# Moving the last stage's weights and images into memory that the routing tables held, and gating its first image in halves

## The chip, the cores and the metric

The program runs on one core of one Trainium2 chip. A core has TensorE (PE in the profile; its weight loads are listed apart as PEld), VectorE (DVE), ScalarE (ACT), GpSimd (POOL) and SyncE (SP), each with its own stream of instructions that it works off in order. They share the on-chip memories SBUF and PSUM, and transfers between SBUF and the device's main memory are made by DMA engines, on orders that SP, ACT or POOL issue. The metric is the device time of one execution in microseconds (us); lower is better.

## What is computed

Two layers follow one another on x of shape (32, 128, 56, 56), in float32.

Layer 0 is a depthwise 7x7 convolution, a normalisation over the channels, and a mixture of 8 experts with 2 experts for each token (a pixel of an image) and a limited number of tokens for each expert. Layer 1 weighs each image with gates along rows and columns, convolves it 3x3 and ends in a SiLU. Cut to what matters here:

```python
# layer 0: x -> depthwise conv -> normalise -> experts
logits = xf @ Wg + bg
topv, topi = jax.lax.top_k(logits, 2)
# each expert takes at most cap = 1.25 * T / 8 tokens, by priority
h = gelu(einsum('ecd,edf->ecf', eb, W1) + b1)
y = einsum('ecf,efd->ecd', h, W2) + b2
x = input + x_skip + layer_scale * moe

# layer 1: gates along h and w, then a 3x3 convolution
x_h = x.mean(3) + x[..., :w // 2].mean(3) + x[..., :w // 4].mean(3)
x_w = x.mean(2) + x[:, :, :h // 2].mean(2) + x[:, :, :h // 4].mean(2)
y = h_swish(bn1d(einsum('ncl,mc->nml', concat([x_h, x_w], 2), w1) + b1))
a_h = sigmoid(einsum('nml,cm->ncl', y[:, :, :h], wh) + bh)
a_w = sigmoid(einsum('nml,cm->ncl', y[:, :, h:], ww) + bw)
out = conv3x3(x * a_w * a_h, wc) + bc
out = out * s2 + (be2 - m2 * s2)
return out * sigmoid(out)
```

## The kernel before

The kernel is written with a framework that lays tiles into memory pools, finds the waits between instructions itself, and orders the instructions of each engine within a stretch of code without branches by its own estimate. A tile of a later pool may lie where a tile of a closed pool was; an instruction that writes it then has to wait until everything that used the old tile is done. So where a tile lies decides how early it can be filled, and the order in the source is not always the order on an engine.

The stages follow one another:

1. The depthwise convolution (line 144), 0 to about 680 us.
2. Normalisation, logits and gates for each token (line 227 and on), to about 1170 us. Each token gets a row in the buffer `acc_d` in main memory.
3. Routing and the experts, to about 3318 us. For each expert a routing of 49 steps on DVE and PE (class `Routing`, lines 370 to 550) finds which rows it takes. Its tables lie in the pool `rc`: work tables for two routings at a time, and for every expert four small results that the experts read later (`new_idx`, line 653). The routing of the later experts is woven into the work of the earlier ones; its last steps are in the fourth expert. An expert works on up to 31 blocks of 512 rows, cut into five chunks (`CHUNKS`). For a block, POOL gathers rows by indirect DMA (line 591), PE transposes them (602), DVE copies them out of PSUM (604), PE multiplies by W1 (612), ACT applies the GELU (613), PE multiplies by W2 (621), ACT and DVE form the rows to be stored (632 to 641), and POOL scatters them to `acc_d` (646). Scatters of a chunk are issued during the next one, gathers one chunk ahead. Chunks after the first stand in a branch that depends on how many rows the expert takes. The weights of expert e + 1 are loaded by SP at the start of expert e (659, 661).
4. The last stage, from about 3318 us to the end. After the last scatter comes a fence: 16 small DVE memsets (line 790), each on a tile that a scatter reads, and every load from `acc_d` waits for them. SP's queue then holds the loads of the weights (`wc` at 820, `w1t` at 835, `wht`, `wwt`, the vectors at 814), the first x (883) and the rows of `acc_d` (891). DVE forms six weight sets `wk` from `wc`, because the 3x3 convolution is done in a transformed way that computes four output rows from six combinations of input rows.

The last stage works on pairs of images. A pair is 49 tiles of 128 tokens, taken in seven groups of seven tiles. `combine` loads the two rows of each token from `acc_d` (`cxn` and `cx`), POOL adds them (894), PE transposes them (900) and DVE adds them to x (902). `squeeze` (915 to 918) reduces each half of an image for the gates. `attend` computes the gates (925 to 945), DVE multiplies the image by them (948, 949) into one of two padded images, `pads`, and POOL and ACT form the six combinations `v` of its rows (956 to 967). `conv` (977 to 990) convolves half an image: 18 matmuls on PE, their combination on DVE, the SiLU and the store on ACT. The convolutions of a pair are spread over the groups of the pair after it. `attend` of the first image comes after the fourth group, that of the second after the seventh.

These pools matter: `cc` holds weights and, before, the two pads; `cx` two buffers for x; `ck` three each for `cxn` and `cx`; `cv` two for `v`.

Of the kernel before, what the change touches and what calls it, by code (L numbers as in the profile page):

```python
# [8 lines left out]
F32 = mybir.dt.float32  # L9
I32 = mybir.dt.int32  # L10
# [3 lines left out]
ALU = mybir.AluOpType  # L14
# [10 lines left out]
P = 128  # L25
NT = T // P
NPAIR = N // 2
# [18 lines left out]
def bc(ap, shape):  # L46
    return ap.to_broadcast(shape)
# [3 lines left out]
def moe_conv_then_coordatt_kernel(ctx: ExitStack, tc: tile.TileContext, a: dict, out: bass.AP):  # L51
# [260 lines left out]
    with ExitStack() as st:  # L312
# [251 lines left out]
        xsp = st.enter_context(tc.tile_pool(name="fs", bufs=2))  # L564
        ptp = st.enter_context(tc.tile_pool(name="fpt", bufs=1, space=PSUM))
# [87 lines left out]
        def new_idx(e):  # L653
            return [rc.tile([P, ST], I32, name=f"idx0_{e}"), rc.tile([P, ST], F32, name=f"idx1_{e}"),
                    rc.tile([1, 1], I32, name=f"taken_{e}"), rc.tile([1, NC_], I32, name=f"parts_{e}")]
# [138 lines left out]
    with ExitStack() as st:  # L794
        cp1 = st.enter_context(tc.tile_pool(name="cc", bufs=1))
        xp = st.enter_context(tc.tile_pool(name="cx", bufs=2))
        kp = st.enter_context(tc.tile_pool(name="ck", bufs=3))
# [36 lines left out]
        nc.gpsimd.memset(w1t, 0.0)  # L834
# [4 lines left out]
        for k in range(4):  # L839
            nc.gpsimd.memset(wq[:, k : k + 1], quarter[k])  # L840
# [14 lines left out]
        def folded(g, be, mean, v, b, n):  # L855
# [5 lines left out]
            nc.gpsimd.memset(mh, -0.5)  # L861
# [12 lines left out]
        for k in range(2):  # L874
            t = cp1.tile([C, H + 2, W + 2], F32, name=f"pad{k}")
            nc.gpsimd.memset(t, 0.0)
            pads.append(t)
# [3 lines left out]
        def load_pair(i):  # L881
            x1 = xp.tile([C, 2, HW], F32, tag="x1", name=f"x1_{i}")
            nc.sync.dma_start(x1, a["x"][2 * i : 2 * i + 2].rearrange("n c h w -> c n (h w)"))
            return x1
# [35 lines left out]
        def attend(i, im, x1):  # L920
# [26 lines left out]
            inner = pad[:, 1 : H + 1, 1 : W + 1]  # L947
            nc.vector.tensor_tensor(img, img, bc(aw.unsqueeze(1), [C, H, W]), ALU.mult)
            nc.vector.tensor_tensor(inner, img, bc(ah.unsqueeze(2), [C, H, W]), ALU.mult)  # L949

            v = vp.tile([C, 6, GR, W + 2], F32, tag="v", name=f"v{nm}")
            d = hp.tile([C, GR, 4, W + 2], F32, tag="d", name=f"d{nm}")
            byq = lambda x: x.rearrange("c (g r) w -> c g r w", r=4)
            low, high = byq(pad[:, 0:H, :]), byq(pad[:, 2 : H + 2, :])
            t = hp.tile([C, GR, 2, W + 2], F32, tag="t", name=f"t{nm}")
            nc.scalar.mul(t, low[:, :, 1:3, :], 4.0)
            nc.gpsimd.tensor_tensor(d, high, low, ALU.subtract)  # L957
            twice = hp.tile([C, GR, W + 2], F32, tag="twice", name=f"twice{nm}")
            nc.scalar.mul(twice, d[:, :, 1, :], 2.0)
            nc.scalar.mul(d[:, :, 0:2, :], d[:, :, 0:2, :], 4.0)  # L960
            nc.gpsimd.tensor_tensor(t, high[:, :, 1:3, :], t, ALU.subtract)
            nc.gpsimd.tensor_tensor(v[:, 1], t[:, :, 1, :], t[:, :, 0, :], ALU.add)  # L962
            nc.gpsimd.tensor_tensor(v[:, 2], t[:, :, 1, :], t[:, :, 0, :], ALU.subtract)
            nc.gpsimd.tensor_tensor(v[:, 3], d[:, :, 2, :], twice, ALU.add)
            nc.gpsimd.tensor_tensor(v[:, 4], d[:, :, 2, :], twice, ALU.subtract)
            nc.gpsimd.tensor_tensor(v[:, 0], d[:, :, 2, :], d[:, :, 0, :], ALU.subtract)
            nc.gpsimd.tensor_tensor(v[:, 5], d[:, :, 3, :], d[:, :, 1, :], ALU.subtract)
            return v
# [25 lines left out]
        todo = []  # L994
        for i in range(NPAIR + 1):
            x1 = load_pair(i) if i < NPAIR else None
# [75 lines left out]
```

## Time and profile before

| What | us |
|---|---|
| median of six runs | 4515.82 (4510.91 to 4523.32) |
| the profiled execution | 4507.24 |
| its span, first to last instruction | 4505.5 |
| experts' stage, first scatter order to last | 1390.1 to 3316.1 |
| first sum of `cxn` and `cx` | 3336.25 |
| first matmul of the last convolution | 3378.44 |
| one pair of the last stage, once settled | about 70.4 |

Busy time over the whole span: PE 3622.5 us (80%), PEld 2351.6 (52%), DVE 2567.3 (57%), POOL 2554.5 (57%), ACT 1410.8 (31%). These shares are means over stages with different limits. From 3400 us to the end PE was busy for 1036.8 of 1105.5 us; in the experts' stage, 1346 to 3308, for 1501.0 of 1962; between 3308 and 3336 not at all. The mean granted clock of PE was 0.89 of full speed.

Lines of the timeline read: start, duration, engine, source line, operation, output and inputs, shapes, number of instructions merged, and in brackets the idle time of the engine just before with what ended it. All times are in us from the start of the span. SPq is SP's queue of DMA orders: its duration is the time of issuing, not of the transfer.

### The profile page before, as it was taken

To read this page: it belongs to the slowest core of one execution; us is meant where nothing else is said; L and a number is where in the kernel's file an instruction comes from. 1 tells how busy PE (TensorE), PEld (TensorE's weight loads), DVE (VectorE), ACT (ScalarE), POOL (GpSimd) and SP (SyncE) were. 2 spreads that over 40 slices of the span, in tenths; PEclk is the share of its full clock that TensorE was granted. 3 is DMA by queue.
4 is the path that set the end of the run, shared out by engine and by line. 5 is a ranking of instruction groups with operands and counts; after the bars stand their busy time and mean duration, and the time that the engine had idled before them with its cause. 6 is when DMAs were issued, how large, how long until landed. Compare 5 with 4: busy or idle time off the path is not lost. (4 is left out here: it accounts for less than half of the span.)

```text
span 4505.5 us, 59987 instructions
## 1 busy us (share of the span) xinstructions
PE 3622.5 (80%) x21360; PEld 2351.6 (52%) x21360; DVE 2567.3 (57%) x5914; ACT 1410.8 (31%) x3132; POOL 2554.5 (57%) x1983
## 2 busy tenths in 40 slices
PE   9999997676318897797788546597858999999999
PEld 4444447666316665565566335465634444544544
DVE  1111115888866966876742212232347888888886
ACT  1111115555203343244243223243412333333332
POOL 1000002322217777668677537777769877877775
PEclk9999998787658898798889778798979999999999
DMA  9999995545362121111111111111155565555652
GB/s 166 222 229 217 229 198 196 214 201 221 149 244 57 49 58 52 45 45 46 52 51 56 50 30 52 56 55 57 56 169 176 168 196 177 182 195 166 196 160 77
DMA packets 814971, 587.33 MB, mean 130 GB/s; under 512 B 545984, under 2 KB 751312, under 8 KB 802128
## 3 DMA queue, kind: packets, MB, share of 16 engines
q1 hardware_dynamic: 508816, 328.72, 25.3%
q10 hardware_dynamic: 262336, 157.84, 12.5%
q0 software_dynamic: 43264, 94.64, 7.3%
q8 instruction: 193, 3.16, 0.3%
q14 instruction: 362, 2.97, 0.2%
HBM read 320.96 MB, written 260.09 MB: 129 GB/s over the span
## 5 line engine op out<-in xcount | busy, mean ns | idle before, releaser
L591 POOL DMA_INDIRECT xg<-acc_d,idx x676 | 673.9, 997 | 406.9 <-issue 181.3
L646 POOL DMA_INDIRECT acc_d<-yo,row x676 | 718.5, 1063 | 234.4 <-issue 81.9
L612 PE MATMUL ph<-fxt,w 128*128 128x512 f32 (+1 forms) x1440 | 700.1, 630 | 53.4 <-ACT ht L613 53.4
L613 ACT ACTIVATE ht<-ph,bias 128x512 f32<-128x512 f32 (+1 forms) x720 | 489.4, 682 | 707.5 <-PE ph L612 706.5
L977 PE MATMUL pc<-v,wk 128*128 128x392 f32 x1920 | 701.0, 507 | 0.4 <-POOL v L962 0.4
L621 PEld LDWEIGHTS py<-w,ht 128*128 128x128 f32 x5728 | 666.8, 193 | 64.8 <-issue 58.2
L621 PE MATMUL py<-w,ht 128*128 128x128 f32 x5728 | 672.4, 277 | 0.0
L144 PE MATMUL acc<-xt,band 56*64 56x424 f32 (+3 forms) x7168 | 668.7, 529 | 2.7 <-POOL band L132 2.7
L977 PEld LDWEIGHTS pc<-v,wk 128*128 128x128 f32 x1920 | 346.8, 191 | 305.9 <-issue 101.1
L144 PEld LDWEIGHTS acc<-xt,band 56*64 56x64 f32 x7168 | 320.3, 133 | 350.4 <-issue 277.5
L227 PE MATMUL lnps<-proj,lnyt 128*128 128x136 f32 x1568 | 354.7, 400 | 138.3 <-ACT sq L232 71.8
L612 PEld LDWEIGHTS ph<-fxt,w 128*128 128x128 f32 x1440 | 279.3, 206 | 328.7 <-issue 241.9
L636 ACT ACTIVATE yo<-xg,own 128x137 f32<-128x137 f32 x716 | 238.1, 401 | 630.0 <-DVE own L632 389.4
L227 PEld LDWEIGHTS lnps<-proj,lnyt 128*128 128x128 f32 x1568 | 349.4, 319 | 144.1 <-ACT sq L232 74.5
L157 DVE TENSOR_SCALAR yt<-acc,dwb 128x448 f32<-128x448 f32 x128 | 87.5, 684 | 584.4 <-PE acc L144 467.2
L639 DVE TENSOR_TENSOR ys<-py,b 128x512 f32<-128x512 f32 (+2 forms) x184 | 123.8, 675 | 491.6 <-PE py L621 481.7
L602 PE MATMUL pt<-ident,xg 128*128 128x128 f32 x716 | 137.1, 312 | 327.4 <-issue 152.2
L132 POOL COPY band<-hk 56x392 f32<-56x392 f32 x128 | 65.3, 510 | 574.4 <-issue 528.2
L987 DVE SCALAR_TENSOR_TENSOR y<-pc,y 128x392 f32<-128x392 f32 x640 | 317.5, 554 | 11.8 <-PE pc L977 11.8
L957 POOL TENSOR_TENSOR d<-pad 128x3248 f32<-128x3248 f32 x32 | 228.0, 7124 | 155.6 <-DVE pad L949 155.6
L894 POOL TENSOR_TENSOR cxn<-cxn,cx 128x896 f32<-128x896 f32 x112 | 260.5, 2334 | 68.2 <-DMA cxn<-acc_d 30.5
L602 PEld LDWEIGHTS pt<-ident,xg 128*128 128x128 f32 x716 | 97.3, 162 | 354.1 <-issue 297.8
(225 smaller groups left out, 4650.9 us busy)
## 6 DMA issues: line engine op xcount, KB each, us to landing
xt<-in_x SPq DMA_DIRECT2D x128, 392.0 KB
y_d<-yt ACTq DMA_DIRECT2D x256, 196.0 KB
lnyt<-y_d SPq DMA_DIRECT2D x16, 3136.0 KB
x<-in_x SPq DMA_DIRECT2D x16, 3136.0 KB
cxn<-acc_d SPq DMA_DIRECT2D x112, 448.0 KB
cx<-acc_d SPq DMA_DIRECT2D x112, 448.0 KB
out<-y ACTq DMA_DIRECT2D x64, 784.0 KB
acc_d<-xn SPq DMA_DIRECT2D x16, 1712.5 KB
```

The source lines that it names most:

```text
L144: nc.tensor.matmul(acc[c][half * G : (half + 1) * G, :, lo:hi], lhsT=band[rows, dw, :], rhs=xt[rows, im, lo + s : hi + s], start=(n == 0), ...
L227: nc.tensor.matmul(ps[:, j, :], lhsT=yf[:, self.j0 + g + j, :], rhs=proj, start=True, stop=True)
L591: d = nc.gpsimd.indirect_dma_start(out=xg[0:n, k, :], out_offset=None, in_=acc_d[0:T1, :], in_offset=bass.IndirectOffsetOnAxis(ap=idx[0][0 ...
L602: nc.tensor.transpose(pt[:, k * P : k * P + n], xg[0:n, k, 0:C], ident[0:n, 0:n])
L612: nc.tensor.matmul(ph[:, 0:N_], lhsT=w[0][:, f * P : (f + 1) * P], rhs=xt[:, 0:N_], start=True, stop=True)
L613: nc.scalar.activation(ht[:, f, 0:N_], ph[:, 0:N_], AF.Gelu, bias=w[2][:, f : f + 1])
L621: nc.tensor.matmul(py[0:n, k, :], lhsT=ht[:, f, k * P : k * P + n], rhs=w2[:, f, :], start=(f == 0), stop=(f == NF - 1))
L636: nc.scalar.activation(yo[0:n, k, :], xg[0:n, k, :], AF.Copy, scale=own[0:n, k : k + 1])
L646: d = nc.gpsimd.indirect_dma_start(out=acc_d[:, :], out_offset=bass.IndirectOffsetOnAxis(ap=row[0:n, k : k + 1], axis=0), in_=yo[0:n, k, : ...
L894: nc.gpsimd.tensor_tensor(xn, xn, x2, ALU.add)
L977: nc.tensor.matmul(m[k], lhsT=wk[k][:, dw, :], rhs=v[:, k, rows, dw : dw + W], start=(dw == 0), stop=(dw == 2))
L987: nc.vector.scalar_tensor_tensor(r[x], m[k], f, r[y_], ALU.mult, ALU.add)
```

## The change

Four things are changed.

- The four small results of a routing move from the pool `rc` to a pool of their own, `fi`, opened after the pools of the experts. The pads move from `cc` to a pool of their own, `cp`, between x and the rows of `acc_d`. With that, `cc` and `cx` lie where the routing's tables and its priorities were, and no longer where the experts' buffers or results are.
- Memsets of the last stage move from POOL to DVE, and only what no other instruction writes is cleared: of `w1t` the columns behind the loaded ones, of each pad its four edges.
- x is asked for a pair ahead: the first pair before the loop, and pair i + 1 at the start of iteration i. There are two buffers for x, as before.
- For the first image of the first pair, the two multiplications by the gates and all that POOL and ACT do for `v` are cut in two halves of output rows (29 and 27 rows of the image, 7 groups of four rows each). For that image the source also has the part from `t` ahead of the differences `d`; for all others the order is as before.

```diff
+        ixp = st.enter_context(tc.tile_pool(name="fi", bufs=1))
...
         def new_idx(e):
-            return [rc.tile([P, ST], I32, name=f"idx0_{e}"), rc.tile([P, ST], F32, name=f"idx1_{e}"),
-                    rc.tile([1, 1], I32, name=f"taken_{e}"), rc.tile([1, NC_], I32, name=f"parts_{e}")]
+            return [ixp.tile([P, ST], I32, name=f"idx0_{e}"), ixp.tile([P, ST], F32, name=f"idx1_{e}"),
+                    ixp.tile([1, 1], I32, name=f"taken_{e}"), ixp.tile([1, NC_], I32, name=f"parts_{e}")]
...
+        padp = st.enter_context(tc.tile_pool(name="cp", bufs=1))
...
-        nc.gpsimd.memset(w1t, 0.0)
+        nc.vector.memset(w1t[:, MIP:QP], 0.0)
...
-            nc.gpsimd.memset(wq[:, k : k + 1], quarter[k])
+            nc.vector.memset(wq[:, k : k + 1], quarter[k])
...
-            nc.gpsimd.memset(mh, -0.5)
+            nc.vector.memset(mh, -0.5)
...
-            t = cp1.tile([C, H + 2, W + 2], F32, name=f"pad{k}")
-            nc.gpsimd.memset(t, 0.0)
+            t = padp.tile([C, H + 2, W + 2], F32, name=f"pad{k}")
+            for edge in (0, H + 1):
+                nc.vector.memset(t[:, edge, :], 0.0)
+            for edge in (0, W + 1):
+                nc.vector.memset(t[:, 1 : H + 1, edge : edge + 1], 0.0)
...
-            inner = pad[:, 1 : H + 1, 1 : W + 1]
-            nc.vector.tensor_tensor(img, img, bc(aw.unsqueeze(1), [C, H, W]), ALU.mult)
-            nc.vector.tensor_tensor(inner, img, bc(ah.unsqueeze(2), [C, H, W]), ALU.mult)
...
+            first = (i, im) == (0, 0)
+            cuts = (0, RP, GR) if first else (0, GR)
+            rows_done = 0
+            for g0, g1 in zip(cuts, cuts[1:]):
+                upto = min(4 * g1 + 1, H)
+                rows = slice(rows_done, upto)
+                n, rows_done = upto - rows_done, upto
+                inner = pad[:, 1 + rows.start : 1 + rows.stop, 1 : W + 1]
+                nc.vector.tensor_tensor(img[:, rows], img[:, rows], bc(aw.unsqueeze(1), [C, n, W]), ALU.mult)
+                nc.vector.tensor_tensor(inner, img[:, rows], bc(ah[:, rows].unsqueeze(2), [C, n, W]), ALU.mult)
+                low, high = byq(pad[:, 4 * g0 : 4 * g1, :]), byq(pad[:, 4 * g0 + 2 : 4 * g1 + 2, :])
+                v, d, t, twice = v_[:, :, g0:g1], d_[:, g0:g1], t_[:, g0:g1], twice_[:, g0:g1]
+                nc.scalar.mul(t, low[:, :, 1:3, :], 4.0)
...
+                def differences():
+                    nc.gpsimd.tensor_tensor(d, high, low, ALU.subtract)
+                    nc.scalar.mul(twice, d[:, :, 1, :], 2.0)
+                    nc.scalar.mul(d[:, :, 0:2, :], d[:, :, 0:2, :], 4.0)
...
+                def first_two():
+                    nc.gpsimd.tensor_tensor(t, high[:, :, 1:3, :], t, ALU.subtract)
+                    nc.gpsimd.tensor_tensor(v[:, 1], t[:, :, 1, :], t[:, :, 0, :], ALU.add)
+                    nc.gpsimd.tensor_tensor(v[:, 2], t[:, :, 1, :], t[:, :, 0, :], ALU.subtract)
...
+                for f in (first_two, differences) if first else (differences, first_two):
+                    f()
+                nc.gpsimd.tensor_tensor(v[:, 3], d[:, :, 2, :], twice, ALU.add)
+                nc.gpsimd.tensor_tensor(v[:, 4], d[:, :, 2, :], twice, ALU.subtract)
+                nc.gpsimd.tensor_tensor(v[:, 0], d[:, :, 2, :], d[:, :, 0, :], ALU.subtract)
+                nc.gpsimd.tensor_tensor(v[:, 5], d[:, :, 3, :], d[:, :, 1, :], ALU.subtract)
...
+        x1s = {0: load_pair(0)}
         for i in range(NPAIR + 1):
-            x1 = load_pair(i) if i < NPAIR else None
+            x1 = x1s.pop(i, None)
+            if i + 1 < NPAIR:
+                x1s[i + 1] = load_pair(i + 1)
```

More of the change, by code (lines that the diff above doesn't have):

```diff
@@ L946, in attend @@
             pad = pads[im]
-            inner = pad[:, 1 : H + 1, 1 : W + 1]
-            nc.vector.tensor_tensor(img, img, bc(aw.unsqueeze(1), [C, H, W]), ALU.mult)
-            nc.vector.tensor_tensor(inner, img, bc(ah.unsqueeze(2), [C, H, W]), ALU.mult)
-            v = vp.tile([C, 6, GR, W + 2], F32, tag="v", name=f"v{nm}")
-            d = hp.tile([C, GR, 4, W + 2], F32, tag="d", name=f"d{nm}")
-            byq = lambda x: x.rearrange("c (g r) w -> c g r w", r=4)
-            low, high = byq(pad[:, 0:H, :]), byq(pad[:, 2 : H + 2, :])
@@ L955, in attend @@
[L955 to L968, printed above, removed]
+            v_ = vp.tile([C, 6, GR, W + 2], F32, tag="v", name=f"v{nm}")
@@ new lines, in attend @@
+            d_ = hp.tile([C, GR, 4, W + 2], F32, tag="d", name=f"d{nm}")
+            t_ = hp.tile([C, GR, 2, W + 2], F32, tag="t", name=f"t{nm}")
+            twice_ = hp.tile([C, GR, W + 2], F32, tag="twice", name=f"twice{nm}")
+            byq = lambda x: x.rearrange("c (g r) w -> c g r w", r=4)
+            first = (i, im) == (0, 0)
[25 more added lines that the diff above has]
+                nc.gpsimd.tensor_tensor(v[:, 5], d[:, :, 3, :], d[:, :, 1, :], ALU.subtract)
@@ L970, in conv @@
+            return v_
         def conv(i, im, ch, v):
```

## The prediction

> **What bounds the kernel now.** I read first the busy time by stretches, to see which stage TensorE (PE) fills. Columns: length, then busy time of PE, PE's weight loads, VectorE (DVE), ScalarE (ACT) and GpSimd (POOL), each with its instructions, the granted PE clock, the DMA share and GB/s.
>
> ```profile
> 3318.00:3336.00 18.00, 0.00 (x0) 0.00 (x0) 10.74 (x34) 0.00 (x0) 6.13 (x4) 0.50 0.69 241
> 3336.00:3357.00 21.00, 14.91 (x74) 8.67 (x74) 10.14 (x20) 1.44 (x2) 14.54 (x7) 0.74 1.05 323
> 3357.00:3383.00 26.00, 12.41 (x47) 6.02 (x47) 21.73 (x16) 5.10 (x8) 18.02 (x6) 0.57 0.52 174
> 3383.00:3400.00 17.00, 11.26 (x37) 6.03 (x35) 6.75 (x8) 1.82 (x2) 17.00 (x8) 0.76 0.34 93
> ...
> 4000.00:4070.50 70.50, 66.52 (x258) 34.87 (x258) 60.13 (x86) 22.88 (x23) 55.80 (x24) 1.00 0.56 183
> ```
>
> The last line is one pair of images in the settled last stage: PE busy for 66.5 of 70.5 us, the others less. So PE bounds that stage, and whatever starts its convolutions earlier should move the end by as much. The first lines are the way there: between the experts' last matmul (3307.4) and 3400, PE does little. The timeline says why (start, duration, engine, line, operation; in brackets the idle time before and what ended it).
>
> ```profile
> 3318.36 0.29 DVE L790 MEMSET yo_end<- 128x4 f32 x3 [7.67 <-DMA acc_d<-yo,row]
> ...
> 3323.46 0.38 SPq L883 DMA_DIRECT2D x<-in_x  x1
> ...
> 3324.43 1.61 SPq L891 DMA_DIRECT2D cx<-acc_d  x1
> ...
> 3336.25 2.07 POOL L894 TENSOR_TENSOR cxn<-cxn,cx 128x896 f32<-128x896 f32 x1 [5.83 <-DMA cx<-acc_d]
> ...
> 3364.99 7.05 POOL L957 TENSOR_TENSOR d<-pad 128x3248 f32<-128x3248 f32 x1 [8.35 <-DVE pad L949]
> ...
> 3376.72 1.66 POOL L962 TENSOR_TENSOR v<-t 128x812 f32<-128x812 f32 x1
> ```
>
> The last scatter lands at 3318.36 and the fence ends at 3318.65. Then SP still issues small loads and the 3.21 MB of x before the first cxn and cx; the first sum starts only at 3336.25. From there it is a chain: squeeze, gates, two DVE multiplications, POOL's `d`, `t` and `v`, and the first conv matmul at 3378.44.
>
> The change also puts work into the fourth expert (weight load for its successor at 2194.88). There I read DVE and PE at the step from its first chunk to its second:
>
> ```profile
> 2254.42 0.16 DVE L633 SCALAR_TENSOR_TENSOR row<-own,idx 128x4 int32<-128x4 f32 x1 [0.95 <-DMA acc_d<-yo,row]
> ...
> 2255.05 0.69 DVE L604 COPY fxt<-pt 128x512 f32<-128x512 f32 x1
> ...
> 2255.83 1.08 PE L602 MATMUL pt<-ident,xg 128*128 128x128 f32 x4 [8.98 <-issue]
> ```
>
> DVE worked without a gap from 2235 to 2252; PE's transposes ended at 2246.85, and it idled 8.98 us until DVE came to the copy. DVE is the limit just there.
>
> **The change, part by part** (the schedule of the changed kernel was read for its order of instructions).
>
> *Loads moved.* wc, w1t, the vectors and the first x now go out during the fourth expert, the second x during the fifth. cxn and cx are then the first things SP issues after the fence: 3318.65 plus two issues of 0.36 to 0.43 gives cx at about 3319.2 in place of 3324.43, -5.2 us. From the issue of cx to its sum took 11.8 us with x ahead of it in the queue; later pairs without it took 4.7 to 5.3 (3341.01 to 3345.74, 3346.50 to 3351.81). That is -6.8, together -12.0. The following sums keep their distance, since without x they came 2.6 to 2.7 us apart, which is 0.92 MB at the 345 GB/s shown there. The steps up to both gates (3357.35) are the same instructions, so these move by -12.0 too.
>
> *Memsets to DVE.* The pads' 5.76 us on POOL lay before the first sum, in its wait for cx. On DVE eight edge memsets (some 0.1 us each, like L790) lie between the fence and the first transposed tile, 5 us later. Nothing either way.
>
> *First image in halves.* The pad was ready 7.2 us after the multiplication began (two of 3.42 and a 0.56 reduction between). Now its first 29 rows are ready after 1.77 + 1.65 + 1.77 = 5.2: -2.0. On POOL the chain to the first `v` was 7.05 + 3.07 + 1.76 + 1.66 = 13.5; no row shows a half-size instruction, but 3248, 1624 and 812 elements took 7.1, 3.1 and 1.7 to 1.9, nearly in proportion, so halves give 3.5 + 1.5 + 0.9 + 0.8 = 6.7: -6.8 (bounds: 0 if size did not matter, -6.8). The second half of the pad is written by DVE just as POOL wants `d`. The trace has a POOL `v` of 1.77 us (L965) stretched to 4.94 at 3379.92, while DVE's L948 ran from 3378.62 to 3383.24; so I let `d` wait those 1.65 us. First conv matmul: -12.0 - 2.0 - 6.8 + 1.7 = -19.1, at about 3359.3.
>
> The Trainium skill says the same more sharply (SBUF — State Buffer, "Who interferes with whom"): a DVE instruction with two SBUF inputs and a GpSimd instruction that reads SBUF exclude each other, and which comes first decides. By it alone POOL's `d`, once started, would hold DVE's second half for its whole 3.5 us, and by the row the loser is POOL; either way the rule speaks against cutting, and the sum differs by about 2 us.
>
> *Given back at once.* In the new order PE does only two conv matmuls, then needs the transposes of the next pair's second group. Their sum stands on POOL behind the first image's second `d`: from 3359.3 on, 0.8 + 0.9 + 1.5 + 0.95 + 0.95 + 0.8 + 0.8 + 3.5 + 2.1 = 12.3, so 3371.7 against 3392.7 before: -21. But before, PE had done six conv matmuls by then, now two; four of them at 0.7 (clock 1.0) to 1.3 us (as at 3378) cost 3 to 5. PE is then some -17, and the second image's gates, which wait for the same transposes, make it -15 to -17. I take -16. Later PE lost 5.1 us once more, at 3450 to 3456 (L942 waiting for DVE's z; DVE waited for ACT, and ACT 15.28 us for POOL's `d` of the next pair). POOL is now further ahead of PE there: 0 to -5, I take -2. From the fourth pair on the order on PE and DVE is as before, so the shift stays. Start of the stage: -18, bounds -13 and -24.
>
> *What the experts' stage pays.* DVE gets 11 weight instructions (4.3 us from 3323.61 to 3327.88), `pick_w` (0.85), wht and wwt (0.3) and seven small memsets (0.4): 5.8 us ahead of the copy at 2255.05. DVE's waits of 0.95 there and 1.88 just after (2260.08) can take up some, so 3 to 5.8; 0 if the delay of PE were made up later. PE passes it to ACT and to POOL's scatters, and POOL ran from 2268.6 to 2511 without a gap over 0.5 us, so I carry +4. DVE also waits for wc there; issued after 2204.15 and 0.59 MB, 2 to 3 us at 345 GB/s, it is in long before 2239. The two loads of x take 9.3 us each at 345 GB/s. PE waited for gathers (4.4 us at 2324, 10.2 at 2406), so a slower gather can show: bounds 0 and 18.6. They use other queues than the gathers, and the DMA share in that stage is 0.18, so I take a value near the low end, +2. SP issues w of the fifth expert before the second x, so no weights wait behind it.
>
> For shared engines the skill (DMA: Bandwidth & Descriptors, "Queues, rings and completion order") has each DMA engine change between queues packet by packet. By that the gathers are slowed, not stopped, nearer +2 than 18.6; no row here shows a gather under such a load.
>
> Sum: -18 + 4 + 2 = -12. The profiled span goes from 4505.5 to 4493.5. That execution took 4507.24, under the lowest of the six timed runs; the median is 4515.82. On the median: 4503.8, so 4504.
>
> **Rivals.** A measurement here tells about 0.2%, 9 us, from no change.
>
> *The gain is paid back in the fourth and fifth expert.* If DVE's 5.8 us go through in full and the loads cost 5, the gain of 18 shrinks to 7: 4509. For it: PE's 8.98 us wait on DVE. Against it: DVE's own waits after it.
>
> *The start gains less.* If POOL's and DVE's exclusion, not the cut, rules the first image (the -6.8 and -2.0 vanish, and only the -12 of the loads stays), then -12 + 6 = -6: 4510. For it: the stretched L965. Against it: nothing long runs on DVE after the second half.
>
> *Slower.* The loads of x hold up the gathers while POOL, without gaps, is what the experts wait for: 18.6 in full, 5.8 of DVE, and the start at its low bound of -13: +11, 4527. It decides as soon as the loads cost more than the start gains less DVE's part, 13 to 24 minus 4. Against it: POOL's issue, not landing, sets the pace (0.95 us each, 0.30 between).
>
> That the change does not do what it says is excluded for the order of the loads; the shift could still end in a longer wait for z.
>
> **Numbers.** Forecast (gain of 9 to 24 us: 4492 to 4507) 0.62; the two cases of a small gain 0.27 together; slower 0.11. The range 4492 to 4518 takes the best start with a free experts' stage (-24) and the low start with DVE in full and 9 us of loads (+2). Faster 0.62, within 0.2% 0.27, slower 0.11.
>
> **What would show it.** Right: cx issued within 1 us of the fence, first sum about 5 us later, first conv matmul some 59 minus 19 = 40 us after the fence instead of 60, with PE idle after two matmuls until the second group's sum; settled pairs again at 70.4 us; the fourth expert 3 to 6 us longer, with the PE wait at its second chunk grown from 9 to about 13. Wrong: settled pairs of another length, experts longer by 10 us or more, or a first sum still 10 us after its load.

## The result, and the profile after

| | kernel before | changed kernel |
|---|---|---|
| median | 4512.61 us (4498.61 to 4525.77, 36 runs) | 4520.06 us (4502.88 to 4532.24, 16 runs) |
| ratio | 1 | 1.0019 (95% interval 1.001 to 1.0028) |
| profiled execution, span | 4505.5 us | 4513.9 us |

The forecast was 4504; the kernel became slower by 0.19%, at the edge of what can be told from no change. Of the prices in the prediction, that of the rival *Slower* (4527) came nearest, but by other terms than its own (loads of x in full, 18.6 us; here at most 5.6), so in part by luck. A sign of being wrong that the prediction named came too: the fourth expert is longer by over 10 us. The question is where the forecast gain of 12 us went.

Busy time of the changed kernel by stretches, each moved by the 16 us by which its fence is late, the settled pair last; columns as in the prediction:

```profile
3334.00:3352.00 18.00, 8.73 (x33) 4.42 (x33) 5.61 (x19) 0.00 (x0) 8.30 (x4) 0.61 0.90 260
3352.00:3373.00 21.00, 9.63 (x57) 5.91 (x56) 17.55 (x19) 2.67 (x4) 10.56 (x5) 0.65 0.85 237
3373.00:3399.00 26.00, 14.96 (x59) 7.51 (x60) 10.09 (x15) 4.50 (x8) 26.00 (x19) 0.63 0.26 71
3399.00:3416.00 17.00, 12.99 (x44) 7.36 (x42) 14.63 (x18) 2.26 (x2) 17.00 (x4) 1.00 0.51 185
4016.00:4086.50 70.50, 65.40 (x245) 34.05 (x244) 56.70 (x76) 22.55 (x22) 55.11 (x23) 0.95 0.56 177
```

PE now has work in the first stretch, where it had none, but POOL has no free moment in the third and fourth: the start is POOL's. The timeline at the same steps:

```profile
3334.37 0.29 DVE L791 MEMSET yo_end<- 128x4 f32 x3 [7.07 <-DMA acc_d<-yo,row]
...
3335.28 0.55 SPq L897 DMA_DIRECT2D cx<-acc_d  x1
...
3340.01 2.06 POOL L900 TENSOR_TENSOR cxn<-cxn,cx 128x896 f32<-128x896 f32 x1 [7.05 <-DMA cx<-acc_d]
...
3370.74 5.04 POOL L975 TENSOR_TENSOR d<-pad 128x1624 f32<-128x1624 f32 x1 [5.19 <-DVE pad L969]
...
3378.26 0.90 POOL L981 TENSOR_TENSOR v<-t 128x406 f32<-128x406 f32 x1
```

The fence ends at 3334.66 in place of 3318.65, 16.0 us late. The first sum comes 5.4 us after it in place of 17.6, as forecast, the `v` that the first convolution reads first 43.6 in place of 58.1. In the fourth expert the step from the first chunk to the second (the last of these rows stood at 8.98 before):

```profile
2262.28 0.16 DVE L634 SCALAR_TENSOR_TENSOR row<-own,idx 128x4 int32<-128x4 f32 x1 [5.38 <-DMA acc_d<-yo,row]
...
2262.90 0.68 DVE L605 COPY fxt<-pt 128x512 f32<-128x512 f32 x1
...
2263.68 1.09 PE L603 MATMUL pt<-ident,xg 128*128 128x128 f32 x4 [16.55 <-issue]
```

DVE stood 5.38 us for a scatter that POOL had not issued in time. Why shows in POOL's queue of DMA orders:

```profile
2244.87 2.89 POOL L647 DMA_INDIRECT acc_d<-yo,row  x1 [0.30 <-issue]
2248.06 7.73 POOL L647 DMA_INDIRECT acc_d<-yo,row  x1 [0.30 <-issue]
2256.09 0.96 POOL L647 DMA_INDIRECT acc_d<-yo,row  x1 [0.30 <-issue]
```

One order took 7.73 us in place of 0.96. Meanwhile DVE of the changed kernel did this (timeline):

```profile
2250.03 0.56 DVE L831 SCALAR_TENSOR_TENSOR wk<-wc,wk 128x384 f32<-128x384 f32 x1
2250.50 0.63 DVE L496 TENSOR_TENSOR bit_r<-bit_r,v_r 128x912 uint16<-128x912 uint16 x1
2251.05 0.36 DVE L833 TENSOR_SCALAR wk<-wk 128x384 f32<-128x384 f32 x1
2251.31 0.63 DVE L497 TENSOR_TENSOR v_r<-v_r,bit_r 128x912 uint16<-128x912 uint16 x1
```

The same place on DVE of the kernel before:

```profile
2250.18 0.63 DVE L496 TENSOR_TENSOR bit_r<-bit_r,v_r 128x912 uint16<-128x912 uint16 x1
2250.85 0.63 DVE L497 TENSOR_TENSOR v_r<-v_r,bit_r 128x912 uint16<-128x912 uint16 x1
```

The weight sets fill in between the steps of the routing, and an instruction starts before the one ahead has ended (2250.03 + 0.56 against 2250.50): DVE has no gap from 2233.8 to 2256.9. Before, the two steps shown leave one of 0.04 us (2250.18 + 0.63 = 2250.81, the next at 2250.85), so the prediction's "without a gap" was nearly right for DVE. POOL's orders at this place in the kernel before:

```profile
2247.31 0.95 POOL L646 DMA_INDIRECT acc_d<-yo,row  x1 [0.30 <-issue]
2248.57 1.39 POOL L646 DMA_INDIRECT acc_d<-yo,row  x1 [0.30 <-issue]
2250.26 1.39 POOL L646 DMA_INDIRECT acc_d<-yo,row  x1 [0.30 <-issue]
```

The long order ended at 2255.79, after the last weight set (2254.05 + 0.36), and without the weight sets it is gone (e1 and g2 below). But a gap on DVE is not by itself what an order needs: the kernel before had none from 2246.20 to 2250.15, and the changed kernel's own orders in the first 11 us of its run took 0.96 to 1.61 us. Nor are long orders new: the third expert of the kernel before has one of 5.17 us (at 2065.69). All orders over 4 us in these traces show one pattern. DVE first runs only steps of the routing, weight sets and sums `yo<-yo,ys`, all of them with every input in SBUF. Then it begins an operation with one input in PSUM (`ys<-py,b`, `fxt<-pt`) or a small one with a single input (`wht`, `own`), and 0.89 to 0.93 us later, about the length of an undisturbed order, the order ends. So the kind of operations in the row seems to count, and the weight sets made that row longer; this is a reading of the traces, and no run tested it.

The fourth expert as a whole, from its load of weights to the next, in the busy time by stretches (length, then PE, PEld, DVE, ACT, POOL), in the kernel before:

```profile
2194.88:2498.03 303.15, 246.19 (x1353) 177.25 (x1354) 141.76 (x322) 120.01 (x246) 222.65 (x222) 0.88 0.19 54
```

And in the changed kernel:

```profile
2194.44:2509.55 315.11, 245.86 (x1353) 177.06 (x1354) 145.94 (x360) 119.75 (x246) 232.28 (x224) 0.86 0.21 64
```

PE worked as long as before (246), POOL 9.6 us longer, and the stretch grew by 12.0.

### The profile page after: what moved, and what is told of

Same layout as the page of the kernel before. It is cut to its first block, busy times and chain, and to the rows that moved or that the text cites. A ratio compares the mean times of both kernels' runs of the same rounds, so it can differ in the third digit from the quotient of the medians.

```text
span 4513.9 us, 59980 instructions
## 1 busy us (share of the span) xinstructions
PE 3625.4 (80%) x21360; PEld 2379.1 (53%) x21360; DVE 2554.8 (57%) x5931; ACT 1411.3 (31%) x3135; POOL 2554.7 (57%) x1982
## 5 line engine op out<-in xcount | busy, mean ns | idle before, releaser
L144 PEld LDWEIGHTS acc<-xt,band 56*64 56x64 f32 x7168 | 347.4, 133 | 324.2 <-issue 261.5
L1009 DVE SCALAR_TENSOR_TENSOR y<-pc,y 128x392 f32<-128x392 f32 x640 | 317.6, 554 | 12.7 <-PE pc L999 12.5
L975 POOL TENSOR_TENSOR d<-pad 128x3248 f32<-128x3248 f32 (+1 forms) x33 | 229.6, 6958 | 152.2 <-DVE pad L969 152.2
```

The source lines that it names most:

```text
L144: nc.tensor.matmul(acc[c][half * G : (half + 1) * G, :, lo:hi], lhsT=band[rows, dw, :], rhs=xt[rows, im, lo + s : hi + s], start=(n == 0), ...
L1009: nc.vector.scalar_tensor_tensor(r[x], m[k], f, r[y_], ALU.mult, ALU.add)
```

## The experiments

Each kernel was timed against the kernel before on the same chip. Five chips took part: the first four kernels, the next four and the last two ran at a mean granted PE clock of 0.89, as the result did; the kernels e9 to e12 and f1 to f4 ran on two chips on which it was 0.85, and where the kernel before takes 5056 to 5070 us. Ratios are compared within a chip.

What the traces say, in us: the fourth expert and POOL's busy time in it, the way from the fifth expert's load of weights to the fence, and the sixth image's gates (end of `attend`, counted from the fence), beyond which the order of work no longer differs and pairs should take about 70.4.

| kernel (clock 0.89) | fourth expert | POOL in it | fifth to fence | sixth gates | ratio, 95% interval |
|---|---|---|---|---|---|
| before | 303.2 | 222.7 | 820.6 | 212.0 | 1 |
| changed | 315.1 | 232.3 | 825.1 | 200.8 | 1.0019 (1.001 to 1.0028) |
| e1, preparation late | 302.0 | 220.4 | 829.2 | 206.1 | 0.9996 (0.9983 to 1.001) |
| e2, x late | 310.7 | 229.5 | 823.7 | 214.1 | 1.0022 (1.001 to 1.0035) |
| e3, no halves | 314.2 | 233.1 | 829.0 | 199.8 | 1.0004 (0.9992 to 1.0015) |
| e4, all three | 302.3 | 220.8 | 823.0 | 209.0 | 0.9993 (0.998 to 1.0006) |
| e5, all moved, whole | 304.1 | 221.6 | 835.3 | 198.5 | 1.0001 (0.9988 to 1.0015) |
| e6, all moved, halves | 301.9 | 219.8 | 836.7 | 198.7 | 1.0004 (0.999 to 1.0018) |
| e7, x in fourth | 301.5 | 219.0 | 831.1 | 198.8 | 0.9993 (0.9978 to 1.0008) |
| e8, sums on PE | 304.5 | 222.7 | 832.1 | 199.9 | 1.0008 (0.9994 to 1.0022) |
| g1, fold moved | 312.5 | 230.6 | 827.8 | 200.4 | 1.0018 (1.0003 to 1.0033) |
| g2, rest moved | 307.9 | 222.4 | 828.9 | 203.5 | 1.0002 (0.9988 to 1.0016) |

### Undoing one part each: e1 to e4

e1: every DVE instruction of the preparation waits for the fence (`after` is the kernel's own way to order two instructions).

```diff
-        nc.vector.tensor_tensor(wk[0], w0, w2, ALU.add)
+        after(nc.vector.tensor_tensor(wk[0], w0, w2, ALU.add).ins, fence[-1])
...
```

> The changed kernel, with VectorE's preparation (the weight combinations, pick_w, the folded scales, the small memsets) made to wait for the fence; its loads and both loads of x stay early. Theory A: back to back, these instructions hold GpSimd off while it issues the fourth expert's scatters (the longest was 7.73 us, against 0.96 usually), and that is 8 of the 16 us by which the fence is late. Then PE's wait at the fourth expert's second chunk goes from 16.6 back to about 9 us, no scatter issue there is over 2.5 us, the fence ends some 8 us earlier than in the changed kernel (about 3326), and the time is 0.15 to 0.2% lower than the changed kernel's, level with the kernel before (ratio 0.999 to 1.001). Theory B: the loads of x are the cause, and the preparation costs only its own 4 to 6 us: the fence 4 us earlier, ratio 1.001. The preparation itself, after the fence, lies in the 5 us wait for the first sum and costs under 1 us by both.

The long order is gone and PE's wait is 8.46 us: that part holds. The fence ends at 3324.2, 7.5 us later than the kernel before's if both are counted from the fourth expert. But behind the fence the preparation cost 5.3 us (sixth gates 206.1 against 200.8), not under 1: the scale of the gates, an 8x1 product on DVE, took 4.57 us while two POOL sums ran, and all later DVE work stood behind it.

e2: x as before.

```diff
-        x1s = {0: load_pair(0)}
...
+            x1 = load_pair(i) if i < NPAIR else None
...
+            if i == 0:
+                for x in fence:
+                    after(d.ins, x)
```

> The changed kernel, with x loaded as before: no pair ahead, and the first one behind the fence; the preparation stays in the fourth expert. Theory A: the first x costs 5 us at the fourth expert's third chunk (PE's wait there 9.5 in the changed kernel, 4.4 before) and the second one 0 to 4 us around the fifth and sixth expert, so the fence ends 5 to 9 us earlier than in the changed kernel, at 3326 to 3330, while PE's wait at the second chunk stays near 16 us; the last stage loses the 6.8 us that x costs ahead of the first sum. Time within 0.05% of the changed kernel. Theory B (x alone is the cause): the fence 12 us earlier, near 3322, ratio to the kernel before 1.0005 at most.

The order of 7.73 us is there again (PE's wait at the second chunk 15.31), and PE's wait at the third chunk is back at 4.59. The fence ends at 3324.1, but the sixth gates (214.1) come later than the kernel before's. Theory A, with 1.0022.

e3: the first image whole.

```diff
-            first = (i, im) == (0, 0)
+            first = False
```

> The changed kernel with the first image in one piece again, in the order differences, then the first two. Nothing changes before the fence. Theory A: from the first d on, GpSimd works without a gap until the second image's d, which sets ScalarE's copy and PE's later wait, so what counts is the sum of GpSimd's work and not its first v: the halves gave an earlier first conv matmul (44.6 us after the fence; in one piece about 50) and nothing at the end: the last stage's length within 2 us of the changed kernel's 1179.2, ratio of the times within 0.05% of the changed kernel's. Theory B, the prediction's: the halves are worth 7 us at the start of the stage, so without them the stage is 1186 and the time 0.15% above the changed kernel's.

The sixth gates come at 199.8, the eighth at 270.4 against 271.5: the halves gain nothing. The stage as a whole took 1189.7 us, because two settled pairs of this execution took 76 to 80 us, of which more below; the median is not above the changed kernel's.

e4: these three together.

> Preparation behind the fence, x as before, the first image in one piece: what is left of the change is that the weights' and vectors' loads go out in the fourth expert, that the tables have a pool of their own, and that VectorE writes only the pads' edges. Theory A: the preparation and x together make up the whole of the 16 us, so the fence ends within 3 us of the kernel before (3316 to 3322), and the last stage gains the 5 us of issues that SP no longer makes ahead of x: ratio 0.9985 to 0.9995. Theory C: something else in the change (pools, order of SP) slows the experts: fence over 3325, ratio 1.000 or more.

The fence ends at 3319.2, within the 3 us, and the gates are 3.0 us ahead. Nothing else in the change slows the experts: theory C falls.

### Placing the parts elsewhere: e5 to e8

```diff
+            turned[e, i] = nc.vector.tensor_copy(xt[:, 0:N_], pt[:, 0:N_]).ins
...
+        after(nc.vector.tensor_tensor(wk[0], w0, w2, ALU.add).ins, turned[E - 2, 2])
...
+            if i < 2:
+                after(d.ins, (turned[E - 2, 0], turned[E - 2, 0])[i])
```

> The changed kernel with the first image in one piece, VectorE's preparation placed behind the third transposed tile of the seventh expert's first chunk (where VectorE is idle for 6 us and GpSimd issues nothing until 12 us later), and both loads of x behind the first tile there. Theory A: preparation and loads cost because of where they fell, so here no scatter issue lasts over 2.5 us, PE's waits in the fourth expert are those of the kernel before (about 8.5 and 5), the way from the fourth expert's load of weights to the fence is within 4 us of the kernel before's 1124 us, and the last stage is 12 us ahead by its eighth gate: the time 8 to 12 us lower, ratio 0.9973 to 0.9982. Theory B: the experts have no room for 6 us of VectorE and 18 us of transfer anywhere: the way to the fence is 10 us longer or more and the ratio 0.9995 or above.

Right for the fourth expert (PE's wait 8.22) and for the gates (198.5; eighth 268.3, 14 ahead), wrong for the sum: the experts after it took 15 us more. Most of that goes with x: from the seventh expert's load of weights to the fence e5 took 687.5 us, e6 688.3 and e8 686.8, but e7 below, which differs from e5 only in that x lies in the fourth and fifth expert, 678.2. So the two loads of x cost some 9 us in the seventh expert. Part was the placement of the preparation. The folded scale needs a POOL operation (the power), which stood in POOL's queue behind 48 orders for gathers, and DVE waited for it in the middle of its queue (e7, same placement):

```profile
2769.81 0.15 DVE L869 TENSOR_TENSOR s_g<-s_g,v_g 8x1 f32<-8x1 f32 x1 [70.07 <-POOL s_g L868]
```

PE stood 64.37 us for the next copy. Yet the 678.2 us of e7 compare with 674.1 in the kernel before and 675.0 to 679.0 in the other kernels without this stop and without x there: a stop of 70 us on DVE cost 4 us at most, while POOL worked on (483.7 us busy against 482.3). In the kernel before, PE waited 16.47 and 19.35 us for gathers in this part, and in e7 not. That is the sharpest sign of who sets the pace among the experts.

> The same with the first image in halves, as in the change. Theory A: GpSimd's sum of work sets the settled lead, so within 2 us of the kernel in one piece either way (0.05%), though the first conv matmul comes 4 to 6 us earlier. Theory B, the prediction's: 7 us better than in one piece, ratio lower by 0.15%.

Sixth gates 198.7 with halves, 198.5 without: theory A.

e7 leaves the loads of x unanchored.

> The kernel with all moved and in one piece, but both loads of x where the change has them, in the fourth and fifth expert. Theory A: they cost 4 to 8 us, seen as a wait of PE for the gathers of 9 us at the fourth expert's third chunk in place of 5, and at the fifth and sixth expert; ratio 0.1 to 0.18% above the kernel with all moved. Theory B (the loads are free, all of the loss was VectorE's): the same time within 0.05%.

The wait is there (8.76 us), and the fourth expert is no longer for it (301.5). The ratio is not higher than that of e5 but, within the intervals, lower. Theory A falls for the first load of x where it lies there without the preparation. With the preparation beside it, it may cost: e2, with x late, took 310.7 us against 315.1.

e8 leaves `combine` of the first pair without POOL's sum:

```diff
+                        for t in (xn, x2):
+                            nc.tensor.matmul(pt[:, j * P : (j + 1) * P], lhsT=t[:, g + j, :], rhs=ident,
+                                             start=(t is xn), stop=(t is x2))
```

> The kernel with all moved and in one piece, and the first pair's seven sums of cxn and cx made on PE, by two accumulating matmuls with the identity in place of a GpSimd sum and a transpose. Theory A (GpSimd and its mutual exclusion with VectorE set the start of the last stage): 2 us off the chain ahead of the first sum, VectorE's gate operations no longer stretched to 1.6 to 2.1 us, and the second image's d 6 to 10 us earlier: the eighth gate 18 to 22 us ahead of the kernel before, the ratio 0.15 to 0.2% below the kernel with all moved. Theory B: PE's extra 12 us (7 times 1.75) lie on the chain and take it back: no gain or up to 12 us lost.

Eighth gates at 270.4: no gain. PE's first wait in the last stage fell from 17.9 (e7; 20.0 in e5) to 14.2 us and some later ones went, and its own 12 us took their place: theory B.

### The clean placement, the doubling, the gates: e9 to e12, f1 to f4

e9 puts the part of the fold behind the power off to the eighth expert (`turned[E - 1, 2]`) and both loads of x behind the last gathers (`turned[E - 1, 22]`).

> First image in one piece; VectorE's preparation in the seventh expert as in the kernels with all moved, but what follows GpSimd's power (scale and offset, for which VectorE waited 70 us there) put off to the eighth expert; both loads of x behind the last gathers, in the eighth expert's fourth chunk. Theory A: none of it costs anything there: from the fourth expert's load of weights to the fence within 4 us of the kernel before's 1124 us, the eighth gate 12 to 14 us earlier after the fence than before's 282.7, ratio 0.9970 to 0.9982. Theory B: the loads or VectorE's work cost wherever they lie: the way to the fence 1130 us or more, ratio 0.9988 or more.

> The same with both loads of x where the change has them (fourth and fifth expert). Theory A: 5 to 8 us longer to the fence than with x behind the last gathers, with the 9 us wait of PE at the fourth expert's third chunk; ratio 0.1 to 0.18% higher. Theory B (x is free there, the preparation was all): within 0.05%.

On this chip e9 has 0.9977 (0.9959 to 0.9995) and e10 0.994 (0.9922 to 0.9958). The eighth gates of e9 are 12 us ahead (270.7). So x early was not dearer, and from the fourth expert's load of weights to the fence e10 took 1354.8 us, e9 1358.3: theory A of e10 (5 to 8 us longer) falls. The distances to the fence can't be held against the other chips'.

e11 makes the weight sets twice:

```diff
+        for again in range(2):
...
```

> The changed kernel with the eleven weight combinations made twice over, 4.3 us more of VectorE in the fourth expert. Theory A (GpSimd can't write its descriptors while VectorE runs on without a gap): the longest scatter issue grows from 7.7 to over 10 us, PE's wait at the second chunk from 16.6 to 20 to 22 us, the fourth expert is 4 to 6 us longer and the ratio 0.1% above the changed kernel's. Theory B (the long issue has another cause and VectorE's work itself is hidden): issue and wait as in the changed kernel, same time.

The longest order took 9.52 us, with 3.94 and 2.89 ahead of it; ratio 1.0052 (1.0032 to 1.0072). The order grew by 1.8 us, not by 4.3. So far theory A, with the size short; the rest does not bear it out. PE's wait at the second chunk is 11.70 us, not 20 to 22, and on another chip of this clock the change as it is has 7.72, 11.11 and a ratio of 1.0068 (f1 below). The change as it is did not run on this chip.

e12 is e9 with the row sums and `z` in PSUM:

```diff
-                               sp.tile([P, 2, SR, 4], F32, tag="rs", name=f"rs{i}_{im}"),
...
+                pa = psp.tile([P, SR * W + L], F32, tag="pa", name=f"cpa{i}_{im}")
+                sums[i, im] = (pa, pa[:, SR * W : SR * W + 8 * SR].rearrange("p (k r q) -> p k r q", k=2, q=4),
...
-            nc.vector.scalar_tensor_tensor(z, r, 6.0, z, ALU.min, ALU.mult)
+            nc.vector.scalar_tensor_tensor(z, r, 6.0, py, ALU.min, ALU.mult)
```

> The kernel with the preparation in the seventh and x in the eighth expert, and in every image the row sums and z kept in PSUM, so that VectorE's short gate operations have at most one operand in SBUF. Same operations and counts. Theory A (they are held off by GpSimd because both operands are in SBUF: 1.8 us on average in the settled stage for work that takes 0.2 to 0.26 where undisturbed): they take 0.2 to 0.4 us, PE's wait of about 1 us for z in each image goes, the settled pair falls from 70.4 to 68.5 to 69.5 us, and the time is 12 to 30 us (0.3 to 0.65%) lower than without. Theory B (VectorE is just busy or the profile stretches them): durations and pairs stay as they are.

0.9943 (0.9926 to 0.996). The durations are as theory A says, the settled pairs are not: 70.2 to 70.4 us. To set these beside the changed kernel, four ran again with it on another chip of the lower clock.

> The changed kernel itself, beside the three that follow on one chip, so that their differences to it need no other chip's times. Theory A (preparation in the fourth expert about 8 us, the loads of x there 4 to 7, start of the last stage -11): ratio 1.001 to 1.0025 to the kernel before. Theory B (the loss seen so far was one chip's): within 0.05% of 1.

> Preparation in the seventh expert, x behind the last gathers in the eighth, first image in one piece. Theory A: nothing is paid among the experts, the 12 us at the start of the last stage stay: 0.25 to 0.4% below the changed kernel on this chip, ratio to before 0.997 to 0.9985. Theory B (work among the experts costs wherever it lies): within 0.1% of the changed kernel.

> The same with x where the change has it. Theory A: 4 to 8 us above the kernel with x behind the last gathers, 0.1 to 0.18%, with PE's 9 us wait at the fourth expert's third chunk. Theory C, from the one chip on which these two ran (there this one was the better by 0.37%): the place of x makes no difference, or the early place is the better one.

> Preparation in the seventh, x in the eighth, gates from PSUM. The run on the other chip showed VectorE's operations at their own length and PE's waits for z gone, but pairs of 70.3 us as before, because PE itself then fills them. So theory A, mended: no shorter pair, but no pair lengthened by 6 to 10 us either, as one to two in a run are without this: 0 to 8 us (0 to 0.18%) below the kernel with x in the eighth. Theory B: the same time within 0.05%.

| same chip, clock 0.85 | fourth expert | fifth to fence | ratio, 95% interval |
|---|---|---|---|
| f1, the change | 407.4 | 979.4 | 1.0068 (1.0045 to 1.0091) |
| f2, x in the eighth | 360.6 | 979.6 | 0.9979 (0.9966 to 0.9992) |
| f3, x in the fourth | 359.7 | 983.1 | 0.997 (0.9954 to 0.9987) |
| f4, f2 with gates from PSUM | 361.9 | 984.9 | 0.9953 (0.9937 to 0.9969) |

f1 missed what was expected of it (1.001 to 1.0025): the change costs more on this chip. With the preparation moved, f2 and f3 are 0.2 to 0.3% faster than the kernel before and 0.9 to 1.0% faster than the changed one; f4 is lowest here, though its interval overlaps those of f2 and f3. On a chip of clock 0.89 these placements did not run. The place of x makes no difference that these runs can tell. The price of the fourth expert's part is 47 us here, four times the 12 us at clock 0.89. POOL's queue in f1:

```profile
2643.94 0.94 POOL L592 DMA_INDIRECT xg<-acc_d,idx  x1 [0.30 <-issue]
2701.09 1.10 POOL L866 TENSOR_TENSOR s_g<-s_g,mh_g 8x1 f32<-8x1 f32 x2 [56.21 <-DVE o_g L868]
2707.29 1.06 POOL L647 DMA_INDIRECT acc_d<-yo,row  x1 [5.09 <-ACT yo L637]
```

The power of the fold stood 56 us for DVE's fold. But the scatters behind it were not ready either: the first waited another 5.09 us for ACT's `yo`. And ahead of the power, with POOL free from 2644.9, all other engines had stood already, for something that the profile does not name ("remote"):

```profile
2650.49 0.69 DVE L640 TENSOR_TENSOR ys<-py,b 128x512 f32<-128x512 f32 x1 [40.15 <-remote]
2650.59 0.69 ACT L614 ACTIVATE ht<-ph,bias 128x512 f32<-128x512 f32 x1 [39.58 <-remote]
...
2651.33 2.08 PE L613 MATMUL ph<-fxt,w 128*128 128x512 f32 x2 [35.88 <-ACT ht L614]
```

In the fourth expert of f1, PE stood 35.88 and 52.80 us in this way, in e11 39.48 and 72.64, in f2, without the preparation, 9.96 and 23.73: the difference between f1 and f2 covers the 47 us. No trace at clock 0.89 has such a wait of over 1 us on DVE or ACT. What ends these stops, and why they are longer with the preparation, stays open. On the first chip POOL came to the power late (2340.72), and DVE waited 12 us for it; with the fold moved away (g1) the fourth expert was less than 3 us shorter.

The groups of the gate operations in the settled stage (shapes, count, busy us, mean ns of one, idle before), in f2:

```profile
L948 DVE SCALAR_TENSOR_TENSOR z<-r,z 8x112 f32<-8x112 f32 x20 | 33.3, 1663 | 0.3
L935 DVE TENSOR_TENSOR rs<-rs,wq 128x56 f32<-128x56 f32 x20 | 30.1, 1504 | 0.0
```

And in f4:

```profile
L948 DVE SCALAR_TENSOR_TENSOR z<-r,cpa 8x112 f32<-8x112 f32 x20 | 5.1, 254 | 0.3
...
L935 DVE TENSOR_TENSOR cpa<-cpa,wq 128x56 f32<-128x56 f32 x20 | 4.5, 224 | 0.7
```

Same work, one operand fewer from SBUF: a sixth of the time. After the eighth gates no pair of e12 and f4 took over 71.3 us, against one of 73 in f2, and one of 73 and two of 77 in f3; one before them in e12 took 73.6. The last stage as a whole was shorter by 12.5 us both times: 1170.8 us in e12 for 1183.3 in e9, 1165.1 in f4 for 1177.6 in f2. Half of that lies ahead of the sixth gates (194.6 for 200.4, 191.2 for 198.8).

### Which part of the preparation: g1 and g2

Both are the changed kernel; g1 moves only the fold, g2 all but the fold, to the places of e9.

> The changed kernel with only the folded scales and offsets (six short VectorE operations each and GpSimd's power) moved to the seventh and eighth expert; weight combinations and the rest of the preparation stay in the fourth, x and halves as in the change. On the chips of the lower clock the changed kernel's GpSimd stood 56 us before the power in the fourth expert, waiting for VectorE's fold. Theory D: that wait is the 45 us between the changed kernel and those with the preparation moved there, so on such a chip this ratio is 0.998 to 1.000; on a chip of the first kind (clock 0.89), where GpSimd came late to the power and had no wait, it stays at the changed kernel's 1.001 to 1.002, with the 7.7 us scatter issue. Theory A (VectorE's run without gaps is all of it): 1.005 or more on a chip of the lower clock.

> The other half: the weight combinations, pick_w and the small memsets in the seventh expert, the folded scales and offsets left in the fourth; x and halves as in the change. Theory D: on a chip of the lower clock GpSimd's wait and the loss stay, ratio 1.004 to 1.007; on a chip of the first kind no scatter issue is over 2.5 us, PE's wait at the fourth expert's second chunk is 8 to 9 us, and the ratio 0.9985 to 1.000. Theory A: below 1.000 on either.

They ran on a chip of clock 0.89. g1 keeps the order of 7.73 us, PE's wait (17.87) and the loss. g2 has no order over 1.61 us in the fourth expert and no loss that its interval can tell, but PE waited 30.82 us at the second chunk, not 8 to 9: without the weight sets ahead of it the fold came early, and DVE waited 22.97 us for POOL's power. Its fourth expert is still 7 us shorter than the changed kernel's, and 5 us longer than that of the kernel before. Which of the two makes the 47 us on the chips of the lower clock was not settled: neither part ran alone there. POOL's 56 us before the power don't settle it, since they may follow from the stops of the other engines.

## Why the prediction was wrong, by its steps

Two terms failed: the +4 for DVE's preparation in the experts' stage, which was 8 to 13 in the fourth expert alone, and the -16 given back at once, of which a wait that was not foreseen left a start of -11 in place of -18.

- *Loads moved, -12.0.* Right. cx is issued 0.6 us after the fence, the first sum comes 5.35 after it (-12.2). The first gates were 9.3 us earlier, not 12: two DVE operations of the gates took 1.87 and 1.64 us beside POOL's sums in place of 0.21 and 0.42. By the sixth gates it was -11.2.
- *Memsets, nothing.* Right; with the tables' pools it is in e4, which lost nothing.
- *First image in halves.* The mechanism was mostly right: the first conv matmul came 44.6 us after the fence, -15.2 for -19.1; `d` lost 1.4 us to DVE (5.04 for 3.60 undisturbed). But it was worth nothing to the stage: e3 and e6 show the same lead without it and with it.
- *Given back at once, -16.* Its end failed, not its beginning. PE's wait for the second group came as foreseen (9.22 us): its transposes began 57.2 us after the fence in place of 74.9, which is the -17 of the text. But a second wait behind it was not foreseen:

```profile
3379.21 2.98 PE L999 MATMUL pc<-v,wk 128*128 128x392 f32 x4 [1.52 <-POOL v L981]
...
3391.91 1.75 PE L906 MATMUL cpt<-ident,cxn 128*128 128x128 f32 x7 [9.22 <-POOL cxn L900]
...
3418.21 1.67 PE L999 MATMUL pc<-v,wk 128*128 128x392 f32 x2 [6.22 <-ACT odd L1004]
```

  ACT's copy of the first convolution stands behind its work on the second image, which waits for POOL's `d`; and POOL had no gap from 3370.7 to 3432. Its sum of work set the lead, and halves do not shorten that sum. Start of the stage: -11 in place of -18, outside the bounds of -13 and -24. The rival "the start gains less" was right in its size, though not in its reason.
- *Experts' stage, DVE's preparation, +4 (3 to 5.8).* The largest miss: 8 to 13 in the fourth expert (e2 against e4, the changed kernel against e1; single executions, and the upper figure has x beside it). The text counted DVE's instructions ahead of the one copy that PE waited for. What counted was POOL: its orders were held, its busy time rose by 9.6, the expert by 12. The prediction had written that POOL runs there without a gap, and carried DVE's figure all the same. The Trainium skill (SBUF — State Buffer, the box on the "DVE blocks DMA" trap in "SBUF: two separate sides") says that GpSimd can't write descriptors while DVE runs an operation in a two-port mode, since the two share a pair of ports. The row of 7.73 us is in line with it, but the trace does not show which operations ran in such a mode. The prediction drew on that page for POOL's arithmetic alone.
- *Loads of x, +2 (0 to 18.6).* Without the preparation beside it the first load cost nothing in the fourth expert (302.0 in e1 with x, 302.3 in e4 without), although PE's wait for the gathers doubled; with the preparation 4.4 (e2). From the fifth expert on, kernels with x early took 825.1, 829.2, 829.0, 827.8 and 828.9, those without 820.6, 823.7 and 823.0: +5.6 by the means of single executions. The medians don't confirm it: those of f2 and f3 are alike within their intervals. Inside the bounds, and its size there stays open; in the seventh expert it was 9 (e5, e6 and e8 against e7).

The sum as the traces have it: +12.0 in the fourth expert and +4.5 from the fifth expert's load to the fence (825.1 against 820.6) make 16.5, of which 0.4 came back before, since the fourth expert's load was issued that much earlier. The sixth gates give -11.2, and what follows them was 3.7 longer (978.5 against 974.8), with some pairs lengthened to 73 us. Together that is, but for rounding, the 8.4 of the spans; the forecast had -12.

## What to carry to other kernels

Before work is moved into an engine's idle time, ask which engine sets the pace there and what the work does to that one: here 6 us on an idle-looking VectorE cost 8 to 13 in the fourth expert, where GpSimd's orders were held up, while a stop of VectorE of 70 us that left GpSimd alone cost 4 at most. In the place where GpSimd sets the pace, a result that crosses engines (VectorE, power, VectorE) needs its inputs long before GpSimd gets to it and its reader long after. And an earlier first matmul was worth nothing here, while the engine that feeds it had no gap: count that engine's whole work up to the settled state.

## What was not expected of the hardware

A short DVE operation can be held off by a whole run of POOL instructions, not only by the one in progress. In e3, one of the two lengthened pairs (start, duration):

```profile
3845.94 7.95 DVE L931 TENSOR_TENSOR rs<-rs,wq 128x56 f32<-128x56 f32 x1
3845.98 1.91 POOL L988 TENSOR_TENSOR v<-d 128x812 f32<-128x812 f32 x1
3847.85 1.92 POOL L989 TENSOR_TENSOR v<-d 128x812 f32<-128x812 f32 x1
3849.72 4.09 POOL L900 TENSOR_TENSOR cxn<-cxn,cx 128x896 f32<-128x896 f32 x2
```

An operation of 0.2 us ended as four POOL instructions had ended (3853.81), and PE waited 7.08 us. The other lengthened pair of e3 has an operation of this kind of 9.99 us (at 4416.3). Why such starts fall where they do is not shown. The Trainium skill (SBUF — State Buffer, "Who interferes with whom") has the lock last for one instruction; these rows show a run of them. What it says of an operation with at most one input from SBUF outside the two-port modes, that it does not contend, is in line with e12 and f4. There is a row beside it, though: `r<-z` (L947), with its one input from SBUF, took 196 to 1841 ns in f2 (median 200), and 252 to 264 in f4, where that input is in PSUM; the trace does not say in which mode it ran.

And the same kernel takes longer on some chips: the changed kernel's profiled execution 4513.9 us where the mean granted clock was 0.89, and 5104.6 where it was 0.85 (f1). The last stage hardly differs (1179.3 and 1186.8 us), the fourth expert does (315.1 and 407.4), and there the stops that end by "remote" stand, of which DVE and ACT have none over 1 us at 0.89. So the clock is not shown to be the cause, which stays open.
